# Four stages of four successive groups emitted side by side in a graph-layer kernel

## The chip, the cores and the metric

The kernel runs on one core of a Trainium2 chip. The metric is the device time of one execution in microseconds (us). Before the change it is 4988.4 us, the median of three runs (4983.2 to 4991.6). PE is the matrix engine (PEld its weight loads), DVE the vector engine, ACT the scalar engine, POOL the GpSimd engine. Each engine has a list of instructions of its own, and in these traces it works through it in the order in which the compiler left it: the text below shows PE waiting 4.55 us at one instruction while the next one could have run.

## The reference

Two layers on 128 graphs of 128 nodes with 256 features, all in fp32:

```python
# layer 0: graph attention twice, then a feed-forward (256 -> 1024 -> 256, relu)
h = _gat(x, adj, W1, a1, Fout)
h = _gat(h, adj, W2, a2, W2.shape[1])
h = _layernorm(residual + h, g_ln1, b_ln1)
ff = relu(h @ w_ff1 + b_ff1) @ w_ff2 + b_ff2
x = _layernorm(h + ff, g_ln2, b_ln2)
# layer 1: attention with 8 heads, values by relation, then a feed-forward (gelu)
attn = softmax(q @ k.T / sqrt(dh))
for r in range(4):
    out += (attn * (adj_matrix == r)) @ v_r
x = _ln(src + out @ Wo + bo, g1, beta1)
ff = gelu(x @ W1 + b1) @ W2 + b2
return _ln(x + ff, g2, beta2)
```

All gains are ones and all shifts zeros in this data.

## The kernel before

Four graphs form a group; 32 groups pass through four stages: the GAT block, the first feed-forward, relational attention, the second feed-forward. Each stage is a Python generator that emits some instructions and yields, and each ends in a layernorm. `together` emits two stages in turns, and the compiler's scheduler then fixes the order on every engine, guided by that sequence. PSUM is the memory in which PE's results arrive; its tiles here are named "mm" (products), "tr" (transposes) and "av" (attention's products with the values). "Filler" below is ready work of another stage.

```python
TB, KB = 4, 6
ps = ctx.enter_context(tc.tile_pool(name="ps", bufs=4, space=PSUM))   # "mm": 4 banks, "tr": 2, "av": 2
# [cut]
def transposed(tok):
    t = wk.tile([P, DC, T], F32, name="T", bufs=TB)
    for c in range(DC):
        p = ps.tile([P, T], F32, name="tr", bufs=2)
        for b in range(G):
            nc.tensor.transpose(p[:, ts(b, N)], tok[:, b, ts(c, P)], ident)
        if c % 2:
            nc.vector.tensor_copy(t[:, c], p)
        else:
            nc.scalar.copy(t[:, c], p)
    return t

def layernorm(y, k):
    mv = sm.tile([P, G, 2], F32, name="mv")
    for b in range(G):
        st = sm.tile([P, 6], F32, name="st")
        nc.vector.bn_stats(st, y[:, b])
        nc.vector.bn_aggr(mv[:, b], st)
    rstd = sm.tile([P, G], F32, name="rstd")
    nc.vector.tensor_scalar(rstd, mv[:, :, 1], EPS, None, op0=OP.add)
    nc.gpsimd.tensor_tensor(rstd, rstd, mhalf, OP.pow)
    for b in range(G):
        nc.vector.tensor_scalar(y[:, b], y[:, b], mv[:, b, 0:1], rstd[:, b:b + 1],
                                op0=OP.subtract, op1=OP.mult)
    nc.gpsimd.tensor_mul(y, y, over_graphs(ln[k][0]))
    nc.gpsimd.tensor_add(y, y, over_graphs(ln[k][1]))
# [cut: the stages; in attention, per relation of a block of four heads:]
    m = wk.tile([P, HC, N], F32, name="m", bufs=5)
    nc.vector.scalar_tensor_tensor(m, ab, float(r), pT, op0=OP.is_equal, op1=OP.mult)
    # [cut: four products m x values into "av"]
# [cut]
(cur,) = together(next_gat(0))
x1, nxt = together(ff0(cur[0]), next_gat(1))
for g in range(NG):
    y, x1_nxt = together(attention(x1, cur[1]), ff0(nxt[0]) if nxt else None)
    y, nxt2 = together(ff1(y), next_gat(g + 2))
    store(g, y)
    x1, cur, nxt = x1_nxt, nxt, nxt2
```

## Time and profile before

| | before |
|---|---|
| span of the profiled run | 4980.2 us |
| busy: PE, DVE, ACT, POOL | 85%, 40%, 30%, 26% |
| mean PE clock | 0.908 |
| one round (mean spacing of the 23 rounds in the middle) | 153.1 us |

The profile's page gives busy shares for the whole run and for 40 slices. The timeline gives single instructions with the idle time of the engine ahead of them and what ended it; the windows view gives busy time by engine and the clock for a stretch. The prediction below shows the lines that matter. In short, PE runs without a gap while two stages with ready work stand side by side, and it idles and then runs slowly where a stage must wait for the layernorm of the stage ahead.

### The profile page before, as it was taken

The page shows a single profiled execution, that of the slowest core. Times are in us where ns is not written, and L with a number is a line of the kernel's source. Part 1 is how long each engine was busy: PE and PEld are TensorE (multiplying, and loading weights), DVE is VectorE, ACT ScalarE, POOL GpSimd, SP SyncE. Part 2 cuts the span into 40 slices and gives each one's busy share as a digit, 9 for nine tenths or more (in the row PEclk, how much of TensorE's full clock was granted, in tenths as well). Part 3 has the DMA queues.
Part 4 walks back from the last instruction along what each step waited for, and adds up shares of the span by engine and source line. Part 5 has one row for each costly group of instructions (what it writes and reads, how often), then busy time and mean ns, then how long its engine had stood idle before and what let it go on. Part 6 is the DMA issues. An engine that isn't in the chain of part 4 may idle for free.

```text
span 4980.2 us, 53267 instructions
## 1 busy us (share of the span) xinstructions
PE 4250.0 (85%) x21144; PEld 2522.2 (51%) x21144; DVE 1973.8 (40%) x4391; ACT 1493.8 (30%) x4184; POOL 1310.4 (26%) x840
## 2 busy tenths in 40 slices
PE   5898888988888988889888898888898888988887
PEld 4455545554544545455554455454454545555444
DVE  2443444433444334444334443344433344433433
ACT  1233232333232332323332223323233232332322
POOL 1222223223222233132222322322322313222232
PEclk8898889998899988999888999889998899988898
DMA  3000000000000000000000000000000000000000
GB/s 96 3 9 11 11 7 7 9 11 11 7 7 9 11 11 7 7 11 9 11 11 7 7 9 11 11 7 7 9 11 11 7 7 11 9 9 5 1 5 9
DMA packets 61384, 53.88 MB, mean 11 GB/s; under 512 B 5584, under 2 KB 60496, under 8 KB 61136
## 3 DMA queue, kind: packets, MB, share of 16 engines
q1 hardware_dynamic: 53312, 46.14, 3.0%
q10 hardware_dynamic: 7824, 4.34, 0.3%
q8 instruction: 166, 2.72, 0.2%
q14 instruction: 82, 0.67, 0.0%
HBM read 33.70 MB, written 16.78 MB: 10 GB/s over the span
## 4 chain that ended last, share of the span: by engine, by line
PE 78%; POOL 8%; DVE 6%; ACT 5%; issue 2%; DMA 1%; ACTq 0%; POOLq 0%; DVEq 0%
PE mm L193 19%; PE mm L183 17%; PE mm L280 9%; PE av L310 6%; PE mm L205 5%; PE mm L288 3%; PE mm L316 3%; POOL tok L171 3%; PE tr L150 3%; PE tr L303 3%; PE mm L263 2%; PE mm L209 2%; PE mm L267 2%; PE mm L251 2%; ACT e L218 2%; POOL tok L170 2%
## 5 line engine op out<-in xcount | busy, mean ns | idle before, releaser
L296 POOL TENSOR_TENSOR e<-e,s 128x512 f32<-128x512 f32 x256 | 266.1, 1039 | 1753.0 <-DVE s L295 1753.0
L308 DVE SCALAR_TENSOR_TENSOR m<-aT,tr 128x512 f32<-128x512 f32 x1024 | 648.7, 675 | 172.0 <-PE tr L303 172.0
L294 ACT ACTIVATE e<-mm,nm 128x128 f32<-128x128 f32 x1024 | 362.8, 367 | 817.0 <-DVE nm L290 816.6
L193 PE MATMUL mm<-wf,fT 128*128 128x256 f32 x2048 | 523.7, 392 | 0.0
L183 PE MATMUL mm<-T,wf 128*128 128x512 f32 x1024 | 508.1, 609 | 0.0
L183 PE MATMUL mm<-T,w 128*128 128x512 f32 x1024 | 497.9, 627 | 0.0
L280 PE MATMUL mm<-wv,T 128*128 128x512 f32 x1024 | 481.7, 602 | 0.0
L310 PE MATMUL av<-m,v 128*32 128x128 f32 x8192 | 435.6, 311 | 50.1 <-DVE m L308 50.0
L193 PE MATMUL mm<-w,fT 128*128 128x256 f32 x2048 | 478.0, 397 | 0.0
L193 PEld LDWEIGHTS mm<-w,fT 128*128 128x128 f32 x2048 | 415.4, 203 | 65.7 <-issue 1.0
L310 PEld LDWEIGHTS av<-m,v 128*32 128x32 f32 x8192 | 197.2, 118 | 452.3 <-DVE m L308 289.1
L193 PEld LDWEIGHTS mm<-wf,fT 128*128 128x128 f32 x2048 | 366.4, 189 | 87.8 <-issue 49.2
L150 PE MATMUL tr<-ident,tok 128*128 128x128 f32 x768 | 131.2, 328 | 298.4 <-POOL tok L171 298.4
L270 ACT ACTIVATE kbd<-mm,bk 32x512 f32<-32x512 f32 x256 | 174.1, 680 | 675.4 <-PE mm L267 672.9
L170 POOL TENSOR_TENSOR tok<-tok,lng 128x1024 f32<-128x1024 f32 x128 | 300.9, 2351 | 193.8 <-DVE tok L168 193.8
L281 DVE TENSOR_TENSOR v<-mm,bv 128x512 f32<-128x512 f32 x256 | 176.4, 689 | 423.5 <-PE mm L280 422.8
L220 POOL TENSOR_TENSOR e<-e,s 128x512 f32<-128x512 f32 x64 | 66.5, 1039 | 1046.9 <-DVE s L219 1046.9
L194 DVE TENSOR_TENSOR tok<-tok,mm 128x512 f32<-128x512 f32 x128 | 88.0, 688 | 630.7 <-PE mm L193 630.7
L183 PEld LDWEIGHTS mm<-T,w 128*128 128x128 f32 x1024 | 207.2, 212 | 216.8 <-issue 215.3
L171 POOL TENSOR_TENSOR tok<-tok,lnb 128x1024 f32<-128x1024 f32 x128 | 300.3, 2346 | 10.0
L185 ACT ACTIVATE fT<-mm,b 128x512 f32<-128x512 f32 x256 | 176.0, 687 | 400.3 <-PE mm L183 399.6
L303 PE MATMUL tr<-ident,e 128*128 128x128 f32 x1024 | 191.4, 302 | 122.3 <-POOL e L296 122.3
(73 smaller groups left out, 5284.4 us busy)
## 6 DMA issues: line engine op xcount, KB each, us to landing
xg<-in_x_dram SPq DMA_DIRECT2D x32, 512.0 KB, 3.8
out_dram<-tok SPq DMA_DIRECT2D x32, 512.0 KB, 2.9
ag<-in_adj_dram SPq DMA_DIRECT2D x32, 256.0 KB, 2.8
wf<-in_L_gnn_w_ff_dram SPq DMA_DIRECT2D x2, 1024.0 KB, 8.9
w<-in_L_gnn_W_dram SPq DMA_DIRECT2D x2, 1024.0 KB, 8.1
wv<-in_L_gnn_Wv_dram ACTq DMA_DIRECT2D x2, 512.0 KB, 9.3
wx<-in_L_gnn_W_dram ACTq DMA_DIRECT2D x2, 256.0 KB, 7.2
bv<-in_L_gnn_bv_dram ACTq DMA_DIRECT2D x1, 512.0 KB, 11.7
```

Of the source, the lines that this page charges most:

```text
L150: nc.tensor.transpose(p[:, ts(b, N)], tok[:, b, ts(c, P)], ident)
L170: nc.gpsimd.tensor_mul(y, y, over_graphs(ln[k][0]))
L171: nc.gpsimd.tensor_add(y, y, over_graphs(ln[k][1]))
L183: nc.tensor.matmul(p, win[:, c, ts(f, P)], hT[:, c], start=c == 0, stop=c == DC - 1)
L193: nc.tensor.matmul(p[:, b - b2_], fT[f][:, ts(b, N)], wout[:, f], start=f == 0, stop=f == FC - 1)
L205: nc.tensor.matmul(p, hT[:, c, ts(b, N)], wx[:, c], start=c == 0, stop=c == DC - 1)
L280: nc.tensor.matmul(p, hT[:, f, ts(b, N)], wv[:, f, r:r + 2], start=f == 0, stop=f == DC - 1)
L294: nc.scalar.activation(e[:, q], p[:, q], AF.Exp, bias=nm[:, q:q + 1], accum_out=s[:, q:q + 1])
L296: nc.gpsimd.tensor_mul(e, e, per_row(s, N))
L303: nc.tensor.transpose(pT[:, q], e[:, q], ident)
L308: nc.vector.scalar_tensor_tensor(m, ab, float(r), pT, op0=OP.is_equal, op1=OP.mult)
L310: nc.tensor.matmul(po[ts(q, DH)], v[:, r, c * P + q * DH:c * P + (q + 1) * DH], m[:, q], start=r == 0, stop=r == R - 1, tile_position=(0, ...
```

## The change

Its intent: take four groups at once, each in another stage, so that every stage's input was finished at least half a step earlier. `together` gets a start, an end and a number of pieces per stage, and emits the piece whose place in the step is lowest. The description says that the stages are spread so that their layernorms end at different times; by the numbers in the diff, though, two end at 0.5 and two at 1.0.

```diff
-    TB, KB = 4, 6
+    TB, KB = 4, 7
[cut: comments removed]
-        aT = wk.tile([P, G, N], F32, name="aT", bufs=3)
+        aT = wk.tile([P, G, N], F32, name="aT", bufs=4)
-                m = wk.tile([P, HC, N], F32, name="m", bufs=5)
+                m = wk.tile([P, HC, N], F32, name="m", bufs=3)
[cut: in together]
+        def when(n):
+            _, steps, begin, end = parts[n]
+            return begin + (end - begin) * live[n] / steps
         while live:
-            for n in list(live):
-                try:
-                    next(live[n])
+            n = min(live, key=when)
+            try:
+                next(parts[n][0])
+                live[n] += 1
[cut: the loop of rounds removed]
+    for s in range(NG + 3):
+        g0, g1, g2, g3 = s, s - 1, s - 2, s - 3
+        got = together(
+            (attention(x1.pop(g2), masks.pop(g2)), 10, 0.0, 1.0) if 0 <= g2 < NG else None,
+            (gat_block(*loads.pop(g0)), 4, 0.0, 0.5) if g0 < NG else None,
+            (ff0(x0.pop(g1)), 7, 0.0, 0.5) if 0 <= g1 < NG else None,
+            (ff1(x2.pop(g3)), 7, 0.5, 1.0) if 0 <= g3 < NG else None,
+        )
[cut: results handed on, store]
```

More of the change, by code (lines that the diff above doesn't have):

```diff
@@ L338, in together @@
         got = [None] * len(parts)
-        live = {n: p for n, p in enumerate(parts) if p is not None}
+        live = {n: 0 for n, p in enumerate(parts) if p is not None}
+        def when(n):
+            _, steps, begin, end = parts[n]
+            return begin + (end - begin) * live[n] / steps
         while live:
-            for n in list(live):
-                try:
-                    next(live[n])
-                except StopIteration as e:
-                    got[n] = e.value
-                    del live[n]
+            n = min(live, key=when)
+            try:
+                next(parts[n][0])
+                live[n] += 1
+            except StopIteration as e:
+                got[n] = e.value
+                del live[n]
         return got
@@ L356, in graph_layers @@
     loads = {0: first_load}
-    def next_gat(g):
-        if g + 1 < NG:
-            loads[g + 1] = load_group(g + 1)
-        return gat_block(*loads.pop(g)) if g < NG else None
-    (cur,) = together(next_gat(0))
-    x1, nxt = together(ff0(cur[0]), next_gat(1))
-    for g in range(NG):
-        y, x1_nxt = together(attention(x1, cur[1]), ff0(nxt[0]) if nxt else None)
-        y, nxt2 = together(ff1(y), next_gat(g + 2))
-        store(g, y)
-        x1, cur, nxt = x1_nxt, nxt, nxt2
+    x0, x1, x2, masks = {}, {}, {}, {}
+    for s in range(NG + 3):
+        if s + 1 < NG:
+            loads[s + 1] = load_group(s + 1)
+        g0, g1, g2, g3 = s, s - 1, s - 2, s - 3
[5 more added lines that the diff above has]
+        )
+        if got[0] is not None:
+            x2[g2] = got[0]
+        if got[1] is not None:
+            x0[g0], masks[g0] = got[1]
+        if got[2] is not None:
+            x1[g1] = got[2]
+        if got[3] is not None:
+            store(g3, got[3])
 _INS = [
```

## The prediction

> **What bounds the kernel now.** I read the page's busy shares first, then the row of granted clock, then the timeline of TensorE (PE) over one whole round, and last the busy time by window.
>
> ```profile
> PE 4250.0 (85%) x21144; PEld 2522.2 (51%) x21144; DVE 1973.8 (40%) x4391; ACT 1493.8 (30%) x4184; POOL 1310.4 (26%) x840
> ...
> PEclk8898889998899988999888999889998899988898
> ```
>
> PE is the only engine near its limit; the second, DVE, is busy 40%. But 85% is no full engine: the clock row lies below 10 in every slice, so part of that busy time is matmuls that run slowly. A slice is 125 us, too coarse to show where; one round of the loop (one group of four graphs) is 154.2 us. In the timeline of PE a round ends and the next begins so (start, duration, line, count, idle before and what ended it):
>
> ```profile
> 2662.74 1.02 PE L288 MATMUL mm<-kbd,T 128*128 128x512 f32 x2
> ...
> 2666.17 0.43 PE L310 MATMUL av<-m,v 128*32 128x128 f32 x8 [0.68 <-DVE m L308]
> ...
> 2670.82 0.59 PE L303 MATMUL tr<-ident,e 128*128 128x128 f32 x2 [3.03 <-POOL e L296]
> ...
> 2681.42 0.70 PE L316 MATMUL mm<-wo,oT 128*128 128x256 f32 x2 [0.38 <-ACT oT L312]
> 2690.86 1.97 PE L150 MATMUL tr<-ident,tok 128*128 128x128 f32 x8 [8.74 <-POOL tok L171]
> ```
>
> PE idles 8.74 us for the attention layernorm (its last GpSimd (POOL) add is L171) because everything next in program order comes after it. Before that the last three of eight head blocks of the attention run with no filler, since the feed-forward beside them was used up. In the second half-round it waits twice more, for the GAT softmax:
>
> ```profile
> 2557.14 2.73 PE L242 MATMUL mm<-e,wh 128*128 128x128 f32 x16 [2.48 <-POOL e L220]
> ...
> 2576.27 3.78 PE L251 MATMUL mm<-wh,e 128*128 128x256 f32 x8 [3.35 <-POOL e L220]
> ```
>
> The windows view splits the round into the second feed-forward with GAT, attention while the first feed-forward lasts, and the rest of attention:
>
> ```profile
> 2537.30:2594.80 57.50, 51.64 (x188) 36.72 (x189) 16.02 (x36) 20.44 (x41) 15.41 (x9) 0.88 0.05 14
> 2594.80:2662.90 68.10, 68.10 (x354) 36.01 (x354) 31.01 (x66) 22.86 (x71) 12.46 (x10) 1.00 0.03 9
> 2662.90:2691.50 28.60, 13.61 (x124) 6.76 (x123) 14.55 (x35) 3.71 (x19) 13.55 (x9) 0.76 0.00 1
> sum 154.20, PE 133.36 PEld 79.49 DVE 61.58 ACT 47.01 POOL 41.42; mean PE 44.45 PEld 26.50 DVE 20.53 ACT 15.67 POOL 13.81
> ```
>
> The first figures are length and PE busy, then PEld, DVE, ACT, POOL, and then the clock. The middle row is the key: 68.1 us, PE busy 68.1, clock 1.00. With attention **and** a filler side by side PE has no gap. The last row has PE busy for under half and a clock of 0.76. So the kernel is bound by PE, plus dependency stalls at stage borders and the slow clock after each.
>
> **What the Trainium skill says.** "TensorE: Matmul & The Clock Gate", Part 1 (The HAM clock gate), says that PE's clock falls to half after an idle window of about 3.4 us and returns after about as much sustained work. The trace agrees: eight transposes last 1.97 us just after the 8.74 us wait and 1.04 us in the dense stretch. "Perfetto Trace Analysis", Optimization Strategy, says that regimes with different limits may gain from interleaving; the 68.1 us row is that. "ScalarE: Activation LUTs", What ACT_TABLE_LOAD costs, gives about 1283 ns for each table load; the groups view has 183 loads of 1283 ns at three lines, so six a round. "PSUM — Partial Sum Buffer" counts 8 banks of 512 fp32 values; the kernel fills them (4 mm, 2 tr, 2 av), so four stages must share what two share now. No row of the trace before shows a lack of them.
>
> **The change part by part.** It removes and adds no arithmetic: it is the same instructions in another order, over 35 steps in place of 32 rounds and a lead-in. In a step attention spans 0 to 1, GAT and the first feed-forward 0 to 0.5, the second feed-forward 0.5 to 1. Their inputs were finished at least half a step before.
>
> (a) **PE work of a full step, dense, at full clock.** Start-to-start times of the timeline: 8 instructions of 512 columns 3.43 us (0.429 each; an fp32 product shows as two), 64 of 256 columns 13.82 us (0.216), 8 transposes 0.87 us. The middle window holds 68.1 us of a round's work. Left of attention: 2 scores (0.86), 12 transposes (1.3), 8 output products (1.7), and 96 av instructions; the 160 av of the middle window are what remains of 68.1 after the others, 9.2 us, so 96 are 5.5. Together 9.4. Second feed-forward: 32 x 0.429 + 64 x 0.216 + 0.87 = 28.4. GAT: 32 x 0.216 + 8 x 0.429 + 16 x 0.108 + 8 x 0.216 + 12 transposes (1.3) = 15.1. One more transposed input of another stage falls into the GAT window: 0.87. Sum 68.1 + 9.4 + 28.4 + 15.1 + 0.9 = **121.9 us**. So of the 154.2 us, 32.3 are loss: 20.8 idle (154.2 - 133.4) and 11.5 slow matmuls.
>
> (b) **What of the loss comes back.** The 8.74 us border wait, the GAT waits, the unfilled end of attention and the slow clock behind them: in each of these places the new order has ready work of another stage. I keep 5 us a step of loss, from two sources. An av block of 8 costs about 0.55 us when other products stand between blocks (0.36, and the next product's 1.05 rather than 0.86), against 0.46 on average in (a): 32 blocks, up to 2.9 us; I take 2. And the layernorms still end in pairs: GAT's with the first feed-forward's at 0.5, attention's with the second's at 1. Each is about 4.1 us of DVE (four of 0.44, of 0.19 and of 0.35) and 5.7 us of POOL (1.02 + 2.35 + 2.35), so a pair is some 8 us of DVE and 11 us of POOL in a burst, while attention's normalisation (L296, 1.04 us) and PSUM evictions queue behind; I take 3 us of PE waits. That makes **127 us** a step.
>
> (c) **Buffers.** aT 3 to 4 and tok 6 to 7 hold the further groups; m falls from 5 to 3 to make room. m has 32 products per round of 0.6 us each on DVE; 3 let DVE run two ahead of PE. Counted in (b), no extra.
>
> (d) **Ends.** Lead-in as now, 141 us to the first attention. Step 2 (no second feed-forward) 121.9 - 28.4 + 4 = 97. Then 29 full steps. Step 32 (no GAT) 121.9 - 15.1 + 2 = 109. Step 33 (attention, 50 of PE work, and 28.4; its first half without filler, and the lone last attention takes 59 us now, 9 more than its work) 85, then 9 of layernorm wait, then the last feed-forward alone, 45 as now. Sum 486.
>
> Total 486 + 29 x 127 = 4169 us of span. The measured time lies about 8 us over the span (4988 to 4980): **4175 us**, a ratio of 0.84.
>
> **Rivals.**
> 1. **Nearly ideal**: PE has no wait at all, 122 to 123.5 a step, 4040 to 4080 us. For it: the 68.1 us stretch without a gap. Against: the paired layernorms and the ends.
> 2. **Bursts on DVE and POOL take the place of the border waits.** For it: the 3.03 us wait for POOL e L296, which arises while POOL works on another layernorm. If each pair costs PE 5 us and the clock dips after it, a step is 135 us: 4410. Against: there was no filler at that spot, now there is.
> 3. **PSUM slots or three m buffers throttle**: transposes share two tr banks with the head blocks, and a bank of scores is held for reduction and four exps. A 4 us delay of each of eight head blocks gives 154 us a step: nothing gained. Against: the middle window has almost this mix in the same banks and no gap.
> 4. **ACT becomes the bound by table loads**: Gelu now runs beside attention's Exp. In the worst case 16 loads a step in place of 6: 13 us on ACT, 47 to 60 of 127. Not the bound; it lengthens attention's chain, which has filler.
> 5. **The throttle lowers the clock under denser work.** Nothing here shows it: 68 us of gapless PE ran at 1.00. The trace has no longer stretch.
>
> **Range and chances.** Rival 1 sets the low end, 4060; the high end is half-way into rival 2, 4350 (133 a step). Same or slower needs rival 3 at nearly full size or rival 5 with a clock of 0.82 throughout: 3% together.
>
> **What would show it.** Right: PE clock 0.97 or more, PE busy 94% or more, DVE near 47%, POOL near 31% of the span; steps of 125 to 129 us; the 8.74 us wait for tok L171 gone but at the end; the GAT waits on e L220 near zero. Remaining waits by the ends of steps and half-steps, on tr or evictions by DVE, would confirm (b). Wrong: clock below 0.93 with PE busy (rival 5), waits on L296 or m L308 all through a step (2, 3), or table loads far above 183 with ACT ahead of PE's waits (4). The prediction fails most easily in the size of (b): I can't see the order in which the instructions of four stages finally stand on each engine.

## The result, and the profile after

The changed kernel takes 4575.0 us (median of four runs, 4574.0 to 4575.8). The ratio to the kernel before is 0.917, with a 95% interval of 0.9157 to 0.9183. A ratio is the mean time of one kernel's fast runs over that of the other's fast runs of the same rounds, so it is not quite the ratio of the medians. The change is faster, as forecast, but by half of what I forecast: 4175 us was predicted, and the result lies above the range of 4060 to 4350. Every kernel gave the right result except one.

| | before | predicted | after |
|---|---|---|---|
| span | 4980 us | 4169 us | 4572 us |
| one round or step | 153.1 us | 127 us | 139.9 us |
| lead-in and end, beside 29 full steps | | 486 us | 515 us |
| mean PE clock | 0.908 | 0.97 or more | 0.948 |

The step is the mean spacing of 23 steps in the middle; 4572 - 29 x 139.9 = 515. Of the 403 us of error in the span, 29 x 12.9 = 374 us are in the full steps. So the question is where 13 us a step go. The same two parts of the page, after:

```profile
PE 4177.7 (91%) x21144; PEld 2398.5 (52%) x21144; DVE 2151.9 (47%) x4391; ACT 1492.3 (33%) x4188; POOL 1311.0 (29%) x840
...
PEclk8899999999999999999999999999999999999999
```

DVE's busy time grew from 1973.8 to 2151.9 us with the same 4391 instructions. That is the first hint: something on DVE became slower. The windows view of one full step of the changed kernel (same columns as before), cut at its two bad places, shows how local the loss is:

```profile
2360.80:2376.00 15.20, 11.09 (x34) 5.94 (x33) 9.81 (x21) 5.75 (x9) 12.07 (x7) 0.78 0.06 18
2376.00:2444.50 68.50, 68.26 (x325) 40.61 (x324) 30.98 (x67) 22.67 (x73) 13.73 (x10) 1.00 0.05 16
2444.50:2456.00 11.50, 6.95 (x42) 2.50 (x42) 7.08 (x12) 4.92 (x12) 10.15 (x6) 0.85 0.01 2
2456.00:2500.40 44.40, 43.29 (x268) 25.51 (x267) 19.57 (x41) 13.55 (x38) 4.90 (x5) 1.00 0.00 1
```

In 113 of the 139.6 us PE is nearly gapless at clock 1.00. The losses sit in 15.2 us at the step's start and 11.5 us in its middle, the two places where two layernorms end together: attention's with the second feed-forward's (end of one step, start of the next), and GAT's with the first feed-forward's. POOL is busiest there: 12.07 of 15.2 us and 10.15 of 11.5 us.

In PE's timeline, the middle of the step looks so (columns as in the prediction):

```profile
2444.55 1.02 PE L185 MATMUL mm<-T,w 128*128 128x512 f32 x2
2450.12 0.66 PE L312 MATMUL av<-m,v 128*32 128x128 f32 x8 [4.55 <-DVE m L310]
2450.71 2.07 PE L185 MATMUL mm<-T,w 128*128 128x512 f32 x2
```

PE waits 4.55 us for an attention mask product `m` from DVE. The feed-forward products of L185 that stand next were free to go, but they stand behind the waiting instruction in PE's order. When they come, two take 2.07 us, against 1.12 us for the same kind later on in this step: in the windows view the clock is 0.50 from 2449.96 to 2453.37. The two at 2450.71 finish a product begun at 2444.55, so nothing that they needed was missing. Why `m` is late is seen in the timeline of DVE and POOL at that place:

```profile
2440.27 2.36 POOL L172 TENSOR_TENSOR tok<-tok,lng 128x1024 f32<-128x1024 f32 x1 [1.50 <-DVE tok L170]
...
2441.76 0.90 DVE L167 TENSOR_SCALAR rstd<-mv 128x4 f32<-128x4 f32 x1
...
2442.72 2.35 POOL L173 TENSOR_TENSOR tok<-tok,lnb 128x1024 f32<-128x1024 f32 x1
2445.03 1.02 POOL L168 TENSOR_TENSOR rstd<-rstd,mhalf 128x4 f32<-128x4 f32 x1
2446.02 2.34 POOL L180 TENSOR_TENSOR tok<-tok,bf 128x1024 f32<-128x1024 f32 x1
2446.08 3.39 DVE L170 TENSOR_SCALAR tok<-tok,mv,rstd 128x256 f32<-128x256 f32 x4 [2.82 <-POOL rstd L168]
2449.39 0.68 DVE L310 SCALAR_TENSOR_TENSOR m<-aT,tr 128x512 f32<-128x512 f32 x1
```

Three things hold DVE up, all from POOL:

- L167, an operation on 128x4 values, takes 0.90 us, where it takes 0.165 us as a mean before. It ends when POOL's L172 ends: 2441.76 + 0.90 = 2442.66, and 2440.27 + 2.36 = 2442.63.
- The second layernorm's power (POOL L168) starts only after the first layernorm's multiplication and addition, so DVE idles 2.82 us for it.
- The four normalisations (L170) that follow take 3.39 us, against 1.38 us without POOL beside them. By the trace the first takes 2.43 us and ends at 2448.51, where POOL's L180 ends at 2448.36; the other three take 0.40 us each, as without POOL.

`m` stands behind them in DVE's order. The skill's page "SBUF — State Buffer", Who interferes with whom, says that a DVE `tensor_scalar` in a two-port mode and a GpSimd operation share one port pair, and that the second to issue is blocked until the first has finished. The end times above agree. So where this text speaks of slow operations beside POOL, it means operations that stood still until one of POOL's had ended. The groups view sums it up; the normalisation before is L168 and after L170, the small addition L165 and L167. Before:

```profile
L168 DVE TENSOR_SCALAR tok<-tok,mv,rstd 128x256 f32<-128x256 f32 x512 | 176.4, 407 | 90.9 <-POOL rstd L166 90.9
...
L165 DVE TENSOR_SCALAR rstd<-mv 128x4 f32<-128x4 f32 x128 | 21.1, 165 | 3.4
```

After:

```profile
L170 DVE TENSOR_SCALAR tok<-tok,mv,rstd 128x256 f32<-128x256 f32 x512 | 313.3, 673 | 165.3 <-POOL rstd L168 165.3
...
L167 DVE TENSOR_SCALAR rstd<-mv 128x4 f32<-128x4 f32 x128 | 94.0, 734 | 1.2
```

These two groups grew by 137 and 73 us, together more than DVE's whole net growth of 178 us (others shrank a little).

At the step's start a second thing is added. In PE's timeline:

```profile
2364.43 0.97 PE L152 MATMUL tr<-ident,xg 128*128 128x128 f32 x4 [2.59 <-ACT aT L232]
...
2366.93 1.12 PE L152 MATMUL tr<-ident,tok 128*128 128x128 f32 x4 [0.68 <-ACT T L156]
2367.84 3.62 PE L185 MATMUL mm<-T,wf 128*128 128x512 f32 x4
2372.30 1.98 PE L185 MATMUL mm<-T,wf 128*128 128x512 f32 x4 [0.84 <-DVE T L154]
```

And in ACT's:

```profile
2361.01 2.76 ACT L272 ACTIVATE kbd<-mm,bk 32x512 f32<-32x512 f32 x4 [2.91 <-PE mm L269]
2363.79 0.59 ACT L232 COPY aT<-tr 128x512 f32<-128x512 f32 x1
```

GAT's next transposes need one of the two `tr` banks. The copy that frees it (aT) stands on ACT behind the four key copies of attention, since attention and GAT both begin at 0.0 and attention is listed first.

### The profile page after: what moved, and what is told of

Same layout as the page of the kernel before. It is cut to its first block, busy times and chain, and to the rows that moved or that the text cites. A ratio compares the mean times of both kernels' runs of the same rounds, so it can differ in the third digit from the quotient of the medians.

```text
span 4571.8 us, 53387 instructions
## 1 busy us (share of the span) xinstructions
PE 4177.7 (91%) x21144; PEld 2398.5 (52%) x21144; DVE 2151.9 (47%) x4391; ACT 1492.3 (33%) x4188; POOL 1311.0 (29%) x840
## 4 chain that ended last, share of the span: by engine, by line
PE 63%; DVE 15%; issue 9%; POOL 9%; ACT 2%; DMA 1%; POOLq 0%; ACTq 0%; DVEq 0%
PE mm L185 17%; PE mm L195 17%; PE mm L282 7%; DVE tok L170 6%; PE av L312 5%; PE mm L290 4%; PE mm L207 3%; POOL rstd L168 3%; DVE m L310 3%; PE mm L211 2%; POOL tok L173 2%; POOL tok L172 2%; ACT kbd L272 2%; PE mm L318 2%; DVE st L164 2%
## 5 line engine op out<-in xcount | busy, mean ns | idle before, releaser
L185 PE MATMUL mm<-T,wf 128*128 128x512 f32 x1024 | 534.8, 666 | 32.4 <-DVE T L154 29.8
L185 PE MATMUL mm<-T,w 128*128 128x512 f32 x1024 | 557.0, 660 | 0.0
L195 PE MATMUL mm<-w,fT 128*128 128x256 f32 x2048 | 515.5, 390 | 0.0
L312 PEld LDWEIGHTS av<-m,v 128*32 128x32 f32 x8192 | 178.6, 112 | 547.2 <-DVE m L310 321.0
L195 PEld LDWEIGHTS mm<-w,fT 128*128 128x128 f32 x2048 | 368.8, 190 | 83.6 <-issue 43.6
L170 DVE TENSOR_SCALAR tok<-tok,mv,rstd 128x256 f32<-128x256 f32 x512 | 313.3, 673 | 165.3 <-POOL rstd L168 165.3
L185 PEld LDWEIGHTS mm<-T,wf 128*128 128x128 f32 x1024 | 209.4, 213 | 299.8 <-issue 223.0
L172 POOL TENSOR_TENSOR tok<-tok,lng 128x1024 f32<-128x1024 f32 x128 | 301.3, 2354 | 164.0 <-DVE tok L170 164.0
L187 ACT ACTIVATE fT<-mm,bf 128x512 f32<-128x512 f32 x256 | 175.6, 686 | 464.3 <-PE mm L185 464.2
L282 PEld LDWEIGHTS mm<-wv,T 128*128 128x128 f32 x1024 | 194.7, 191 | 249.7 <-issue 241.6
L292 DVE TENSOR_REDUCE nm<-mm 128x4 f32<-128x512 f32 x256 | 176.6, 690 | 263.7 <-PE mm L290 263.7
```

The source lines that it names most:

```text
L185: nc.tensor.matmul(p, win[:, c, ts(f, P)], hT[:, c], start=c == 0, stop=c == DC - 1)
L195: nc.tensor.matmul(p[:, b - b2_], fT[f][:, ts(b, N)], wout[:, f], start=f == 0, stop=f == FC - 1)
L282: nc.tensor.matmul(p, hT[:, f, ts(b, N)], wv[:, f, r:r + 2], start=f == 0, stop=f == DC - 1)
L292: nc.vector.tensor_reduce(nm, p, AX.X, OP.max, negate=True)
L312: nc.tensor.matmul(po[ts(q, DH)], v[:, r, c * P + q * DH:c * P + (q + 1) * DH], m[:, q], start=r == 0, stop=r == R - 1, tile_position=(0, ...
```

## The experiments

Theory A: layernorms that end in pairs hold DVE through POOL, PE waits behind DVE, and its clock drops. Theory B: the three `m` buffers throttle. Theory C: at a step's start ACT's order holds a transpose bank. Twelve kernels ran; the table gathers them.

| run | median us | ratio to before | step us |
|---|---|---|---|
| the change | 4575.0 | 0.917 | 139.9 |
| apart | 4575.6 | 0.917 | 139.9 |
| noaffine | 4268.9 | 0.856 | 130.8 |
| attlater | 4401.2 | 0.882 | 134.3 |
| before_m3 | 4986.9 | 0.999 | |
| midapart | 4366.0 | 0.875 | 133.1 |
| nopow | 4463.7 | 0.895 | 136.5 |
| normact | 4679.2 | 0.938 | 143.4 |
| spread | 4250.8 | 0.852 | 129.7 |
| mid_later | 4174.9 | 0.837 | 127.0 |
| spread2 | 4247.8 | 0.852 | 129.7 |
| spread_tact | 4111.7 | 0.825 | 125.1 |
| spread_noaffine | 4090.8 | 0.821 | 125.5 |

### apart: all four layernorms end at different places

```diff
-(gat_block(...), 4, 0.0, 0.5)    (ff1(...), 7, 0.5, 1.0)
+(gat_block(...), 4, 0.0, 0.3)    (ff1(...), 7, 0.4, 0.85)
```

> Only the spans of the stages in a step change: GAT ends at 0.3, the first feed-forward at 0.5, the second (from 0.4) at 0.85, attention at 1.0, so no two layernorms end at the same place. Theory A (pairs: the second layernorm's power and its normalisation wait on POOL, which works for the first; DVE is held, PE waits and its clock halves): the 4.56 us wait on m in mid-step goes, most of the 7.9 us loss at the step's start too, the four normalisations fall back from 3.40 to about 1.4 us; a step 139.6 -> about 129 us, total 4250 to 4350 us. Theory B (three m buffers): unchanged, 4575. Theory C (step start: the aT copy sits behind four key copies on ACT and two transpose banks): only the mid-step part is gained, 6 us a step, 4400.

It measured 4575.6 us, no gain at all, and by the number alone theory A would fall. The profile says otherwise. The groups view shows DVE's small addition back at 165 ns and the normalisation at 449 ns:

```profile
L170 DVE TENSOR_SCALAR tok<-tok,mv,rstd 128x256 f32<-128x256 f32 x512 | 203.6, 449 | 139.2 <-POOL rstd L168 139.2
...
L167 DVE TENSOR_SCALAR rstd<-mv 128x4 f32<-128x4 f32 x128 | 21.1, 165 | 3.3
```

The 4.55 us wait in mid-step is gone from PE's timeline. But at the end of the step, others have come:

```profile
2482.23 0.42 PE L312 MATMUL av<-m,v 128*32 128x128 f32 x8 [0.72 <-DVE m L310]
...
2491.06 0.69 PE L305 MATMUL tr<-ident,e 128*128 128x128 f32 x2 [2.93 <-POOL e L298]
```

The second feed-forward now ends at 0.85, so the last head blocks of attention have no filler, just as in the kernel before. In the windows view the last 22 us of the step run with 16.43 us of PE work at a clock of 0.84. One gain and one loss of the same size cancelled. The experiment changed two things, and taught me to move one end at a time.

### midapart: only GAT's layernorm moved

```diff
-(gat_block(...), 4, 0.0, 0.5)
+(gat_block(...), 4, 0.0, 0.4)
```

> Only the GAT stage ends earlier, at 0.4 instead of 0.5, so that its layernorm no longer meets the first feed-forward's; the pair at the step's end and every filler stay. Theory A (a pair costs the wait on m and the slow clock after it): the 4.56 us wait in mid-step and its clock loss go, 6 us a step: 4400, range 4370 to 4440. If the layernorms' pairing is not the cause in mid-step: within 1% of 4575.

It measured 4366.0 us, 209 us less than the change from one number in the source, and just under the range expected. No wait on `m` appears in mid-step, and the step falls by 6.8 us to 133.1. This is the cleanest test of theory A: the pair in mid-step is the cause of the loss there. The number moves all of GAT's pieces a little, so the test doesn't stand alone: noaffine below leaves every piece in its place, and there too the wait falls, to 0.25 us.

### attlater: attention begins just after GAT

```diff
-(attention(...), 10, 0.0, 1.0)
+(attention(...), 10, 0.02, 1.0)
```

> Attention starts at 0.02 instead of 0.0, so at a step's start the GAT transposes and their ACT copies stand ahead of attention's query and key products. Theory C: the 2.59 us wait of PE on aT (ACT does four key copies, 2.76 us, first) goes, and part of the cold clock after it: 3 to 5 us a step, total 4430 to 4490. Theory A alone (start loss is only DVE held by layernorms): the wait moves elsewhere, within 1% of 4575.

It measured 4401.2 us, 174 us less; that is 29 us under the range expected. The wait on aT at the step's start falls from 2.59 to 0.18 us:

```profile
2403.19 0.33 PE L152 MATMUL tr<-ident,xg 128*128 128x128 f32 x1 [0.18 <-ACT aT L232]
```

The clock of the first 19 us of the step is 1.00, where the first 15 us had 0.78. Theory C holds for the start; the wait of 4.55 us on `m` in mid-step stays. That theory A has a part at the start too is supported by noaffine, which keeps the wait on aT and yet gains more than midapart.

### before_m3: the kernel before with three m buffers

```diff
-m = wk.tile([P, HC, N], F32, name="m", bufs=5)
+m = wk.tile([P, HC, N], F32, name="m", bufs=3)
```

> The kernel before with three m buffers instead of five, the one part of the change that takes something away. Theory B (three m buffers throttle DVE and PE): slower than before by 1 to 4%. Theory A: m is used up at once by PE in order, 4988 within 0.5%.

It measured 4986.9 us, a ratio of 0.999 (0.9968 to 1.0011). In the kernel before, three buffers cost nothing. Five in the changed kernel were not tried. That midapart removes the wait on `m` with three buffers speaks against theory B there too.

### noaffine: gain and shift on POOL left out

```diff
-nc.gpsimd.tensor_mul(y, y, over_graphs(ln[k][0]))
-nc.gpsimd.tensor_add(y, y, over_graphs(ln[k][1]))
```

> The two POOL operations with gain and shift at the end of each layernorm are left out (the gains are ones and the shifts zeros in this data, so the result stays right here, but not in general). This takes 18.8 us of POOL work from a step. Theory A: mid-step wait and DVE part of the start loss go, normalisations 3.40 -> 1.4 us for four; total about 4330. Theory B (m buffers): no change in the mid-step wait on m; total within 1% of 4575. Theory C: the 2.59 us wait on aT at the step start stays in any case.

It measured 4268.9 us, 306 us less than the change and 61 us less than expected. The result is right only because the gains are ones and the shifts zeros. The wait on `m` in mid-step falls to 0.25 us, while the wait on aT at the start stays at 2.58 us, as both theories said of their own part. The step falls by 9.1 us to 130.8, more than the 6.8 us of midapart.

### nopow: the power on POOL left out

```diff
-nc.vector.tensor_scalar(rstd, mv[:, :, 1], EPS, None, op0=OP.add)
-nc.gpsimd.tensor_tensor(rstd, rstd, mhalf, OP.pow)
+nc.vector.tensor_scalar(rstd, mv[:, :, 1], 0.0, 0.7, op0=OP.mult, op1=OP.add)
```

> Wrong result on purpose: the reciprocal root on POOL is left out and a constant factor 0.7 taken instead, so that DVE never waits for POOL in a layernorm; POOL's multiplications and additions stay. It parts two ways in which POOL holds DVE: the queue (2.83 us in which the normalisation waits for the power behind POOL's other work) and the slow execution (3.40 us for four normalisations instead of 1.38, 0.90 us for a 128x4 operation instead of 0.17). If the queue is the larger part: mid-step wait under 2 us, total 4380 to 4460. If slow execution beside POOL is enough: mid-step wait still over 2.5 us, total over 4480, and L170 stays above 600 ns mean.

The result is wrong, with a relative error of 0.61. It measured 4463.7 us and fell between the two forecasts: the mid-step wait is 2.3 us. DVE no longer waits for the power, but it then starts the normalisations sooner, beside POOL, and they take longer still:

```profile
2383.26 2.35 POOL L172 TENSOR_TENSOR tok<-tok,lnb 128x1024 f32<-128x1024 f32 x1
2383.72 5.11 DVE L169 TENSOR_SCALAR tok<-tok,mv,rstd 128x256 f32<-128x256 f32 x4
2385.69 2.34 POOL L179 TENSOR_TENSOR tok<-tok,bf 128x1024 f32<-128x1024 f32 x1
...
2389.47 0.43 PE L311 MATMUL av<-m,v 128*32 128x128 f32 x8 [2.30 <-DVE m L309]
```

The four end at 2388.83, 0.80 us after POOL's second operation (2388.03), with 5.11 us in place of 1.38. So the wait is about halved without POOL's power (2.30 for 4.55 us), and what is left comes from normalisations that stand still beside POOL. The two are not simply added: removing one exposes part of the other.

### normact: the normalisation on ACT

```diff
-    nc.vector.tensor_scalar(y[:, b], y[:, b], mv[:, b, 0:1], rstd[:, b:b + 1],
-                            op0=OP.subtract, op1=OP.mult)
+nb = sm.tile([P, G], F32, name="nb")
+nc.vector.tensor_scalar(nb, mv[:, :, 0], -1.0, None, op0=OP.mult)
+nc.gpsimd.tensor_mul(nb, nb, rstd)
+    nc.scalar.activation(y[:, b], y[:, b], AF.Identity, bias=nb[:, b:b + 1], scale=rstd[:, b:b + 1])
```

> The normalisation goes from DVE to ACT (scale and bias per row; the bias is made by one small DVE operation and one more POOL operation of about 1 us). Then DVE has nothing that waits for POOL's power. Theory A: mid-step wait on m goes or falls under 1 us although the layernorms end in pairs; ACT gets about 6 us more a step, POOL 4 us more. The ACT wait at step start may grow. Total 4380 to 4480. If DVE is not the link between POOL and PE: within 1% of 4575.

It measured 4679.2 us, slower than the change, where I expected a gain. DVE's small operations are back at 0.16 us and PE no longer waits on `m`. But ACT's order is as fixed as DVE's:

```profile
2497.38 1.00 POOL L168 TENSOR_TENSOR rstd<-rstd,mhalf 128x4 f32<-128x4 f32 x1
...
2500.67 0.19 POOL L171 TENSOR_TENSOR nb<-nb,rstd 128x4 f32<-128x4 f32 x1
...
2500.90 2.07 ACT L173 ACTIVATE tok<-tok,nb,rstd 128x256 f32<-128x256 f32 x4 [3.91 <-POOL nb L171]
...
2503.60 2.83 PE L187 MATMUL mm<-T,w 128*128 128x512 f32 x4 [2.04 <-ACT fT L189]
```

ACT now idles 3.91 us for POOL, and PE waits for an activation behind it. At the step's start two such normalisations stand ahead of the aT copy, and PE waits 7.58 us for it. The wait moved with the instruction. What counts is that an engine that evicts PSUM waits for POOL, not which one it is.

### spread: places meant to part the layernorms, with filler to the end

```diff
-attention 0.0, 1.0    gat 0.0, 0.5    ff0 0.0, 0.5     ff1 0.5, 1.0
+attention 0.02, 0.95  gat 0.0, 0.4    ff0 0.0, 0.55    ff1 0.5, 1.05
```

> All four layernorms apart and filler kept to the end: GAT to 0.4, first feed-forward to 0.55, attention 0.02 to 0.95, second feed-forward 0.5 to 1.05. The step before showed that parting the layernorms by ending the second feed-forward at 0.85 leaves attention's last head blocks alone. Theory A plus C plus filler: step about 127 us, total 4170 to 4270. If parted ends always cost as much as they bring: 4400 or more.

It measured 4250.8 us, inside the expectation, but only the mid-step's pair came apart. At the step's start PE still waits 2.39 us for a transposed copy on DVE. The timeline there shows the small addition beside POOL once more:

```profile
2449.68 2.41 POOL L173 TENSOR_TENSOR tok<-tok,lnb 128x1024 f32<-128x1024 f32 x1
...
2450.47 1.65 DVE L167 TENSOR_SCALAR rstd<-mv 128x4 f32<-128x4 f32 x1
```

It ends at 2452.12, and POOL's addition, of attention's layernorm, at 2452.09: attention's layernorm and the second feed-forward's still meet. `together` uses the places only to sort the pieces, and between these two layernorms it emits one piece, half of an output product.

### mid_later: the two single edits together

```diff
-attention 0.0, 1.0    gat 0.0, 0.5
+attention 0.02, 1.0   gat 0.0, 0.4
```

> Both single edits that helped, together and nothing else: GAT ends at 0.4, attention starts at 0.02. Alone they took 209 and 174 us off 4575. If the mid-step loss and the step-start loss are separate: 4192, range 4170 to 4220. If they share a cause: 4280 or more.

It measured 4174.9 us. The two losses are separate: 209 + 174 = 383 us were expected, and 400 came. This happens to be the time that I had predicted for the change itself. The pair at the step's end still meets here, but DVE's transposed copies (2405.96 and 2406.64) stand ahead of the small addition that waits for POOL (2407.22), where in spread two of them come behind it. A whole step in the windows view has PE busy 123.71 of 127.00 us at clock 1.00:

```profile
2397.20:2524.20 127.00, 123.71 (x662) 72.98 (x661) 60.95 (x139) 46.78 (x131) 40.76 (x26) 1.00 0.04 11
```

### spread2: attention's end moved further from the last layernorm

```diff
-attention 0.02, 0.95   ff1 0.5, 1.05
+attention 0.02, 0.86   ff1 0.5, 1.0
```

> As spread, but attention ends at 0.86 and the second feed-forward at 1.0, so that attention's layernorm lies some 18 us of the step ahead of the last one instead of 13, and its POOL additions are over before the last one's statistics. Theory A: the 1.65 us small DVE operation and the 2.39 us wait on DVE's transposed copy at the step's start get shorter; 4180 to 4240. If only the second feed-forward's own layernorm matters there: within 0.5% of spread, 4251.

It measured 4247.8 us, within 0.1% of spread: theory A's forecast missed. But the edit didn't do what was meant. Sorted by their places, the last pieces of a step come in the same order as in spread (attention's layernorm, one piece of the second feed-forward, its layernorm), and the trace shows the pair where it was:

```profile
2440.96 1.02 POOL L168 TENSOR_TENSOR rstd<-rstd,mhalf 128x4 f32<-128x4 f32 x1 [14.87 <-DVE rstd L167]
2445.93 2.41 POOL L173 TENSOR_TENSOR tok<-tok,lnb 128x1024 f32<-128x1024 f32 x1
2446.73 1.65 DVE L167 TENSOR_SCALAR rstd<-mv 128x4 f32<-128x4 f32 x1
2448.86 1.02 POOL L168 TENSOR_TENSOR rstd<-rstd,mhalf 128x4 f32<-128x4 f32 x1
```

The two powers (L168) start 7.90 us apart, in spread 7.89. The second feed-forward's small addition still ends (2448.38) with attention's last addition on POOL (2448.34), and PE still waits 2.40 us on DVE's transposed copy. So this run doesn't clear attention's layernorm. Its other forecast (only the second feed-forward's own layernorm matters) was met by the time but isn't shown; spread_noaffine below speaks against it. In mid-step a wait of 1.53 us on `m` came, where spread has 0.37 us. The run also shows that the slow clock doesn't follow every such wait. In two successive steps:

```profile
2321.46 2.08 PE L265 MATMUL mm<-T,wq 128*128 128x512 f32 x2 [2.40 <-DVE T L154]
...
2452.55 1.13 PE L265 MATMUL mm<-T,wq 128*128 128x512 f32 x2 [2.40 <-DVE T L154]
```

### spread_tact: all transposed copies on ACT

```diff
-            if c % 2:
-                nc.vector.tensor_copy(t[:, c], p)
-            else:
-                nc.scalar.copy(t[:, c], p)
+            nc.scalar.copy(t[:, c], p)
```

> As spread, but both halves of every transposed input are copied out of PSUM by ACT, none by DVE. At the step's start PE waits 2.39 us for such a DVE copy behind the last layernorm. Theory A: this wait goes, PE's clock there stays up: 2 to 4 us a step, 4140 to 4200. If ACT's queue then makes PE wait as it did with the normalisation on ACT: 4251 or more.

On top of spread, it measured 4111.7 us, 28 us under the range expected and the fastest kernel here with general results: a ratio of 0.825 to before, and 10% less than the change. A step takes 125.1 us. This copy needs nothing from POOL, and on ACT it doesn't stand behind a layernorm. The pair at the step's end still meets (the small addition takes 2.12 us there), but PE no longer waits behind it.

### spread_noaffine: the limit without POOL's additions

The diff is that of noaffine, on top of spread.

> As spread, without gain and shift on POOL (right for this data only). In the changed kernel this took 306 us off. Theory A: spread has already removed most of what POOL's additions cost inside a step, so at most 100 us is left to gain, of it about 10 us per lone stage at the ends: 4150 to 4230. If POOL's additions cost in some other way than by meeting other layernorms: 300 us again, 3950.

It measured 4090.8 us, 160 us less than spread, where I expected at most 100. My expectation took the layernorms in spread to be apart. At the step's end they are not, so POOL's gain and shift still cost there: without them the small addition takes 0.15 us in place of 1.65, the wait on DVE's copy falls from 2.39 to 0.48 us, and the step from 129.7 to 125.5 us; 29 x 4.2 = 122 us of the gain is there. Like noaffine it is right for this data alone.

## Why the prediction was wrong

**Part (a), the dense work of a step, was right.** I derived 121.9 us and 2 us for isolated head blocks, 123.9 together. The best step measured, in spread_tact, is 125.1 us with nearly no waits. The round of the kernel before is 153.1 us by mean spacing, not the 154.2 of my window, which was cut 0.7 us too long; nothing rests on that.

**The step that failed is the last term of part (b)**, the sentence "I take 3 us of PE waits". A full step takes 139.9 - 123.9 = 16 us beyond what (a) and the isolated blocks account for, where the term says 3. About 14 of them lie in the two bad windows. The start window holds 20 transposes, 8 instructions of L185 and 4 of query products, some 7.3 us of dense work by the rates of part (a), in 15.2 us. The middle one holds some 5.5 us in 11.5 us. Sum of losses: 7.9 + 6 = 14; some 8.7 of it is idle time (15.2 - 11.1 and 11.5 - 7.0), the rest slow products. I had the right event in the text (pairs of layernorms, some 8 us of DVE and 11 us of POOL in a burst), but sized it wrongly for four reasons:

- I took DVE's durations from the kernel before. Beside POOL, four normalisations take 3.39 us rather than 1.38 and the small addition 0.90 rather than 0.165. The views of before could not show it, since there POOL's and DVE's parts of different layernorms did not meet so.
- I wrote of "ready work of another stage" as if PE could take it. It was there, but behind the waiting instruction in PE's fixed order.
- I left the slow clock out of the 3 us. After the 4.55 us wait the next two products took 2.07 us instead of 1.12.
- I did not foresee the tie at 0.0, where attention's key copies stand ahead of GAT's aT copy on ACT; attlater shows it worth 174 us.

**Part (d), the ends,** was 29 us short (515 for 486). Step 2, the first with attention, took 113.8 us where I had 97. No run tested this, but its trace shows waits of the same kinds as a full step's: 4.09 us on `m`, 2.58 on aT and 2.43 on POOL's e are the longest.

**The rivals.** Rival 2 (bursts on DVE and POOL take the place of the border waits) is what happened, at 135 us a step by my own sizing and 139.9 measured. I gave it too little weight because of the filler. Rival 3: three `m` buffers cost nothing in the kernel before (before_m3), and the wait on `m` in the change goes without more of them (midapart); two `tr` banks do play a part at the step's start, through ACT's order. Rival 4: the groups view has 187 table loads at the two lines of feed-forward and attention and one more, against 184 in all before; it is refuted. Rival 5: PE ran at 1.00 over 68.5 us in the change and over 127 us in mid_later; it is refuted. **Rival 1** was nearly reached only by spread_tact and spread_noaffine.

**The signs that I named.** The wait on tok L171 and the GAT waits are gone from full steps, as said. PE's share is 91%, not 94%, and the clock 0.948, not 0.97. "Remaining waits by the ends of steps and half-steps" came true for the places; but in mid-step the wait is on `m`, not on tr or an eviction, and the size was far off.

In total, waits and slow clock weigh alike: from the change to mid_later the span falls by 399 us, PE's busy time for the same 21144 instructions by 195 (4177.7 to 3982.8), and its idle time by 204. What stays open: how this divides within each pair, since no run removed the slow clock and left the wait; and what the pair at the step's end costs a kernel in which it is really parted, since only apart parted it, and that run took filler from attention.

## What to carry to other kernels

When several stages are interleaved, look at where their tails on the slow shared helper engines coincide. In mid-step, two bursts that ended at the same place cost the busy engine far more than the same work apart: one number in the schedule was worth 209 us of 4575. Ready work is no filler if it stands behind a waiting instruction in an in-order queue; so before counting on it, ask what each evicting engine waits for. A schedule edit that moves two ends can cancel its own gain, as in apart, or leave the order as it was, as in spread2; only the profile shows that.

## What the Trainium skill lacked or had wrong

- "SBUF — State Buffer", Who interferes with whom: the rule is there and agrees with the trace, but without what it means for a small operation and for a third engine. A 128x4 DVE addition took 0.90 and 1.65 us beside POOL against 0.165 us alone. The page says of ports that PE and ACT never wait on anyone; through DVE's queue, PE waited 4.55 us for such a blocked operation.
- "TensorE: Matmul & The Clock Gate", Part 1, names a free-running idle window of about 3.4 us as what slows the clock. It lacks how little work makes a window idle. In spread2 a wait of 2.40 us was followed by a slow product in one step (2.08 us for two), and by a fast one in the next (1.13 us). By the windows view the 3.41 us before the slow stretch still held 1.35 us of PE work, and the clock was then 0.50 for 3.42 us; in the next step, cut at the same spacing, they held 2.06 and 1.68 us, and the clock stayed at 1.00.
- "Perfetto Trace Analysis", Optimization Strategy, advises interleaving regimes. It lacks the caution that the tails of interleaved stages may meet: 139.9 us a step with pairs, 133.1 with one pair parted, 127.0 with the start's tie removed too.
